# Last FFN of a decoder: quantisation cut in two steps, its scales on GpSimd, a bf16 last product, and the norm taken by halves

## The chip, the cores and the metric

The kernel is one program on 1 core of one Trainium2 chip. The metric is the time of one execution on the device, in microseconds; the figure for a kernel is the median of several runs. The kernel before took 2508.41 us (three runs, 2505.84 to 2514.92).

## The reference, cut to what matters

The model is a decoder of four layers, each with self-attention, cross-attention and an FFN, on 8 batches of 112 tokens with 256 features. The change touches the last FFN, in which inputs, weights and the hidden values are rounded to a 4-bit format with a scale for every 16 neighbouring elements:

```python
def fake_quant_nvfp4(x, global_scale):
    xb = x.reshape(sh[:-1] + (sh[-1] // BLOCK, BLOCK))          # BLOCK = 16
    amax = jnp.max(jnp.abs(xb), axis=-1, keepdims=True)
    sc = jnp.clip(amax / FP4_MAX * global_scale, 0.0, FP8_MAX)
    sc8 = sc.astype(jnp.float8_e4m3fn).astype(jnp.float32)
    dq = sc8 / global_scale
    safe_dq = jnp.where(dq == 0.0, 1.0, dq)
    a = jnp.clip(jnp.abs(xb) / safe_dq, 0.0, FP4_MAX)
    q = jnp.sign(xb) * _FP4_VALS[jnp.digitize(a, _FP4_MIDS)]
    return (q * dq).reshape(sh)
...
gate_out = nvfp4_linear(x, gate_w, s_in[0])                      # 256 -> 1024
up_out = nvfp4_linear(x, up_w, s_in[0])                          # 256 -> 1024
hidden = jax.nn.silu(gate_out) * up_out
return nvfp4_linear(hidden, down_w, s_in_down[0])                # 1024 -> 256
...
x = x + _L3_xattn_ref(_layernorm(x, axis=-1), ctx_512, L3_xattn_Wq, L3_xattn_Wkv, L3_xattn_Wo)
x = x + _L3_ffn_ref(_layernorm(x, axis=-1), L3_ffn_gate_w, L3_ffn_up_w, L3_ffn_down_w, L3_ffn_s_in, L3_ffn_s_in_down)
```

## The kernel before

The program runs the twelve sublayers one after the other on one core. The residual `x` stays in on-chip memory (SBUF) with the 112 tokens on partitions and (batch, feature) along the row. Each sublayer is written batch by batch or half by half (a half is four batches). Python code emits the instructions; a scheduler then sets the order on each engine by its own estimates, except on engines named in a `manual_schedule` block, where the order of the code stands. Every engine works through its own queue in order and waits on semaphores for the others. `self.t(pool, ..., tag)` takes a buffer from a pool; a tag has as many buffers as its pool's `bufs`, so a new one waits until the oldest is free.

The parts that matter here:

- `quantise` (from L1807) rounds `n` columns of `src` into `dst`. For each block of 16 columns it takes the largest magnitude (L1824), and then makes the scale from it in nine small instructions on n/16 columns: scale and clip (L1826, L1827), rounding to fp8 by masking the exponent and adding and subtracting a large number (L1831, L1834 to L1836), a guard against zero (L1837), the reciprocal (L1838) and its product with the global scale (L1840). Seven passes over all `n` columns follow: the quotient (L1843), clip (L1844), rounding (L1846 to L1849), and the product with the scale (L1850). All of it is on VectorE. A block's 16 elements are neighbours in the row.
- `l3_weights` (from L1852) does the same with the three weight matrices, in six calls on 1024 columns. It is a generator that `l2_ffn` (from L1607) advances while its own matmuls run; the rounded matrices are transposed on TensorE (L1884) and kept in bf16. Their raw values come by DMAs from GpSimd's queue (L1860). In `l2_ffn` VectorE also makes the gated product `hT` (L1625).
- `l3_xattn` (from L1798) is the cross-attention in front of the last FFN. It calls `cross` (from L950), whose order on TensorE, VectorE and ScalarE is written by hand. At the end of a batch it adds the result to `x` (L455).
- `l3_ffn` (from L1899): the norm of all of `x` (L1916, whose instructions carry the lines of the helpers `stats`, `rsqrt` and `normalise`: L402, L403, L385 to L392, L416), then for each half `quantise` on 1024 columns into `xq`, eight transposes (L1926), and a copy of the result to SBUF on ScalarE (L1931). After this comes a loop over four pairs of batches. For each pair, four times (two batches, two blocks of 512 columns): four matmuls into one `gu` buffer (a PSUM tile of which there are two; line L378 of the helper `mm`), Silu on ScalarE into `sg` (L1942), and the gated product into `hid` on VectorE (L1943). The pair's 2048 columns of `hid` are rounded into `hq` by one call of `quantise` (L1948), and for each batch eight transposes (L1952), a copy on ScalarE to `hqT` (L1956), eight matmuls into `y` (L378) and the sum with `x` (L1960) follow. Nothing in `l3_ffn` has an order by hand: the scheduler mixes pairs.
- `store` (L1963) writes `x` out with one DMA.

## Time and profile before

| what | before |
|---|---|
| runs, median (lowest to highest) | 2508.41 us (2505.84 to 2514.92) |
| the profiled execution's own time | 2510.18 us |
| its span, from first to last instruction | 2508.4 us |
| TensorE (PE) busy | 2223.4 us, 89% |
| VectorE (DVE) busy | 1460.0 us, 58% |
| ScalarE (ACT) busy | 834.6 us, 33% |
| GpSimd (POOL) busy | 212.9 us, 8% |
| granted TensorE clock, mean | 0.933 |
| last sum of the layer before the last FFN ends (L455) | 2384.4 us |
| last sum of the last FFN ends (L1960) | 2502.5 us |

The profile is one execution taken by the hardware profiler. It names engines PE (TensorE matmul), PEld (TensorE weight load), DVE (VectorE), ACT (ScalarE), POOL (GpSimd) and SP. Times are microseconds from the first instruction, durations in the group rows are mean nanoseconds. In a group row the first number is the total busy time, the second the mean of one instruction, and the last part is how long the engine sat idle just before such instructions and what ended that wait. Tiles have the names of the program. A row of the waits view reads: who waited, for whom, total us, number of times, longest.

### The profile page before, as it was taken

What the parts mean: (1) busy time and instruction counts of PE and PEld (TensorE: products, weight loads), DVE (VectorE), ACT (ScalarE), POOL (GpSimd) and SP (SyncE); (2) the same over time, 40 slices, a digit from 0 to 9 for tenths busy, and PEclk for the clock granted to TensorE, in tenths of its full rate; (3) what the DMA queues carried; (4) which work ended last, traced back from release to release, by engine and by line L of the source; (5) the groups of instructions that cost most, each with busy time, mean ns of one, the idle gap of its engine ahead of it and who ended that gap; (6) DMA issues with size and microseconds to landing.
All of it is one profiled execution on the core that took longest, in us unless ns stands there. A gap on an engine that the chain in (4) does not pass through costs nothing.

```text
span 2508.4 us, 43509 instructions
## 1 busy us (share of the span) xinstructions
PE 2223.4 (89%) x17192; PEld 1343.6 (54%) x17192; DVE 1460.0 (58%) x3879; ACT 834.6 (33%) x2276; POOL 212.9 (8%) x412
## 2 busy tenths in 40 slices
PE   6999999989989889999998887899999999799942
PEld 3444444657655656655666444456655556556622
DVE  4555656555544656763588664767660042656698
ACT  2333333111221246751012122367521111356621
POOL 0111111000001110000112231100000000100000
PEclk9999999786899999999999997999999999899966
DMA  4000001000010000001000001000111000000000
GB/s 182 2 2 2 2 19 63 1 17 1 17 51 1 14 18 2 18 18 42 34 1 34 18 18 59 34 2 1 52 51 50 35 17 1 1 1 2 2 0 15
DMA packets 10731, 56.42 MB, mean 22 GB/s; under 512 B 1833, under 2 KB 3625, under 8 KB 5536
## 3 DMA queue, kind: packets, MB, share of 16 engines
q1 hardware_dynamic: 8304, 45.03, 5.0%
q0 software_dynamic: 2080, 7.07, 0.8%
q8 instruction: 137, 2.24, 0.4%
q10 hardware_dynamic: 144, 1.54, 0.1%
q14 instruction: 66, 0.54, 0.1%
HBM read 52.69 MB, written 0.92 MB: 21 GB/s over the span
## 4 chain that ended last, share of the span: by engine, by line
PE 67%; DVE 21%; issue 5%; ACT 4%; DMA 1%; POOL 1%; DVEq 0%; ACTq 0%; POOLq 0%
PE mm L378 33%; PE gu L378 6%; PE g L612 6%; PE tr L1031 6%; PE sc L378 5%; PE av L378 3%; PE av L1047 2%; DVE xnm L1021 2%; DVE rot L1326 1%; ACT sg L623 1%; PE s L378 1%; ACT th L634 1%; DVE hT L638 1%; PE tr L477 1%; DVE h L636 1%
## 5 line engine op out<-in xcount | busy, mean ns | idle before, releaser
L612 PE MATMUL g<-w,hT 128*32 128x256 f32 x3552 | 237.4, 384 | 25.8 <-DVE hT L638 24.4
L1024 ACT ACTIVATE xe<-sc,xnm 112x375 f32<-112x375 f32 x384 | 215.6, 580 | 29.1 <-DVE xnm L1021 29.1
L1031 PEld LDWEIGHTS tr<-cst,xe 112*125 112x125 f32 x1152 | 157.2, 187 | 108.8 <-ACT xkT L982 30.0
L378 PE MATMUL mm<-xnT,w 128*128 128x448 f32 x432 | 191.3, 580 | 20.3 <-DVE qT L1329 4.5
L1031 PE MATMUL tr<-cst,xe 112*125 112x112 f32 x1152 | 197.8, 291 | 11.4 <-DVE xoT L1074 6.5
L1021 DVE TENSOR_REDUCE xnm<-sc 112x1 f32<-112x375 f32 x384 | 184.4, 541 | 29.2 <-PE sc L378 29.0
L378 PE MATMUL mm<-hT,w 128*128 128x448 f32 x512 | 193.0, 539 | 0.0
L612 PEld LDWEIGHTS g<-w,hT 128*32 128x32 f32 x3552 | 95.7, 109 | 167.5 <-DVE hT L638 124.6
L1039 DVE COPY xeT<-tr 125x336 f32<-125x336 f32 x192 | 97.4, 507 | 98.1 <-PE tr L1031 90.5
L378 PEld LDWEIGHTS mm<-hT,w 128*128 128x128 f32 x512 | 97.1, 190 | 94.4 <-issue 94.4
L378 PEld LDWEIGHTS mm<-xnT,w 128*128 128x128 f32 x432 | 80.5, 199 | 109.1 <-issue 55.8
L590 PE MATMUL g<-xw,cst 128*32 128x256 f32 x1792 | 138.7, 379 | 0.0
L378 PE MATMUL mm<-w,oT 128*112 128x256 f32 x416 | 119.8, 445 | 21.2 <-DVE oT L1506 13.7
L378 PE MATMUL mm<-w,hT 128*112 128x256 f32 x576 | 132.6, 389 | 0.0
L1037 ACT COPY xeT<-tr 125x336 f32<-125x336 f32 x192 | 85.3, 444 | 127.6 <-PE tr L1031 127.6
L378 PE MATMUL gu<-xnT,w 128*128 128x448 f32 x320 | 124.4, 544 | 1.7 <-DVE hT L1171 1.2
L378 PEld LDWEIGHTS mm<-w,hT 128*112 128x112 f32 x576 | 103.6, 182 | 27.6 <-issue 4.9
L378 PEld LDWEIGHTS mm<-w,oT 128*112 128x112 f32 x416 | 82.9, 208 | 52.4 <-DVE oT L1506 14.9
L623 ACT ACTIVATE sg<-g 128x192 f32<-128x192 f32 x224 | 74.2, 331 | 105.2 <-PE g L612 93.4
L634 ACT ACTIVATE th<-cell 128x64 f32<-128x64 f32 x224 | 57.7, 258 | 147.0 <-DVE cell L632 146.9
L455 DVE TENSOR_TENSOR x<-mm,x 112x256 f32<-112x256 f32 x64 | 27.1, 423 | 126.2 <-PE mm L378 126.2
L636 DVE TENSOR_TENSOR h<-sg,th 128x64 f32<-128x64 f32 x224 | 50.4, 225 | 84.9 <-ACT th L634 84.9
(375 smaller groups left out, 3744.5 us busy)
## 6 DMA issues: line engine op xcount, KB each, us to landing
w<-in_w SPq DMA_DIRECT2D x35, 1024.0 KB, 4.9
raw<-in_wq POOLq DMA_DIRECT2D x3, 1024.0 KB, 5.2
wi<-in_wint POOLq DMA_DIRECT2D x3, 768.0 KB, 5.9
w<-in_w SPq DMA_DIRECT2D x2, 896.0 KB, 16.6
w<-in_w SPq DMA_DIRECT2D x2, 768.0 KB, 4.1
ctxT<-in_ctxT ACTq DMA_DIRECT2D x1, 1500.0 KB, 7.8
cx<-in_ctx POOLq DMA_DIRECT2D x1, 1500.0 KB, 20.9
w<-in_w SPq DMA_DIRECT2D x2, 512.0 KB, 3.5
```

The costliest lines, as they stand in the source:

```text
L378: self.nc.tensor.matmul(out, lhsT, rhs, start=i == 0, stop=i == len(pairs) - 1)
L590: nc.tensor.matmul(g[32 * j : 32 * j + 32, :], pick[:, t % 16, :], xw[:, l, t // 16, 256 * j : 256 * j + 256], start=True, stop=t == 0, sk ...
L612: nc.tensor.matmul(g[32 * j : 32 * j + 32, :], hT[l][:, c, :], whh[l][:, c, 256 * j : 256 * j + 256], start=False, stop=c == 1, skip_group ...
L623: nc.scalar.activation(sg[:, :192], g[:, :192], AF.Sigmoid)
L634: nc.scalar.activation(th, cell[l], AF.Tanh)
L636: nc.vector.tensor_tensor(h, og, th, ALU.mult)
L1021: nc.vector.tensor_reduce(nm, sc, AX.X, ALU.max, negate=True)
L1024: nc.scalar.activation(e, sc, AF.Exp, bias=nm, accum_out=sums[b][:, at : at + 1])
L1031: nc.tensor.transpose(tp[:CH, i * S : (i + 1) * S], e[:, i * CH : (i + 1) * CH], self.ident[:S, :S])
L1037: nc.scalar.copy(eT, src)
L1039: nc.vector.tensor_copy(eT, src)
L1047: nc.tensor.matmul(avs[b][32 * j : 32 * j + 32, c * S : (c + 1) * S], values[b % 2][:CH, i, 4 * c + j, :], eTs[b, c, j][:, i, :], start=i ...
```

## The change

`quantise` becomes a generator with one stop in the middle: the first step makes the scales, the second does the passes over all columns. Of the small instructions the two that scale and clip, three of the four that round to fp8, and the last product with the global scale go to GpSimd, which also makes a copy of the scale in bf16; the exponent mask, the zero guard and the reciprocal stay on VectorE. The results of the passes are stored with a row's blocks interleaved ("at a pitch"): element e of all blocks, then element e+1. The same is done to the weights, so that the matmuls contract in the same permuted order. The last subtraction then writes bf16, and the product with the scale has only bf16 operands, with the scale repeated along the middle axis. The signs of the subtraction are turned round on both sides.

In `l3_ffn` the norm is taken half by half, just ahead of that half's quantisation. The loop over pairs becomes two functions: `hidden(b0)` makes `hid` and runs the first step of its quantisation, `result(b0)` runs the second step and the down projection. VectorE's order in this loop is written by hand: the hidden values and scales of the next pair, then the sums that are left of the last pair, then the quotient of the present one.

```diff
--- before.py
+++ after.py
@@ -1804,50 +1804,60 @@
             )
         w.done("l3x_wo")
 
-    def quantise(self, pool, src, dst, rows, n, gs, amax=None):
+    def quantise(self, pool, src, dst, rows, n, row, gs, amax=None, small=None):
 
 
         nc = self.nc
         nb = n // 16
 
-        def blocks(a):
-            return a.rearrange("p (k e) -> p k e", e=16)
+        def inner(a):
+            return a.rearrange("p (r e k) -> p r e k", e=16, k=row // 16)
 
         def bc(a):
-            return a[:, :, None].to_broadcast([rows, nb, 16])
-        def sm(tag):
-            return self.t(pool, [P, nb], f"q{tag}{nb}")[:rows]
+            return a.rearrange("p (r k) -> p r k", k=row // 16)[:, :, None, :].to_broadcast(
+                [rows, n // row, 16, row // 16]
+            )
+        def sm(tag, dt=F32):
+            return self.t(small or pool, [P, nb], f"q{tag}{nb}", dt)[:rows]
 
         if amax is None:
             amax = sm("m")
-            nc.vector.tensor_reduce(amax, blocks(src), AX.X, ALU.max, apply_absolute_value=True)
-        sc, st, z = sm("s"), sm("t"), sm("z")
-        nc.vector.tensor_scalar(sc, amax, 1.0 / 6.0, gs, ALU.mult, ALU.mult)
-        nc.vector.tensor_scalar(sc, sc, 448.0, None, ALU.min)
+            blocks = src.rearrange("p (k e) -> p k e", e=16)
+            nc.vector.tensor_reduce(amax, blocks, AX.X, ALU.max, apply_absolute_value=True)
+        sc, st, z, s16 = sm("s"), sm("t"), sm("z"), sm("h", BF16)
+        nc.gpsimd.tensor_scalar(sc, amax, 1.0 / 6.0, gs, ALU.mult, ALU.mult)
+        nc.gpsimd.tensor_scalar(sc, sc, 448.0, None, ALU.min)
 
 
         big = 1.5 * 2.0**23
         nc.vector.tensor_scalar(
             st.bitcast(I32), sc.bitcast(I32), 0x7F800000, None, ALU.bitwise_and
         )
-        nc.vector.tensor_scalar(st, st, 0.125 * big, 2.0**-9 * big, ALU.mult, ALU.max)
-        nc.vector.tensor_tensor(sc, sc, st, ALU.add)
-        nc.vector.tensor_tensor(sc, sc, st, ALU.subtract)
-        nc.vector.scalar_tensor_tensor(z, sc, 0.0, sc, ALU.is_equal, ALU.add)
+        nc.gpsimd.tensor_scalar(st, st, 0.125 * big, 2.0**-9 * big, ALU.mult, ALU.max)
+        nc.gpsimd.tensor_tensor(sc, sc, st, ALU.add)
+        nc.gpsimd.tensor_tensor(sc, st, sc, ALU.subtract)
+        nc.gpsimd.tensor_copy(s16, sc)
+        nc.vector.scalar_tensor_tensor(z, sc, 0.0, sc, ALU.is_equal, ALU.subtract)
         nc.vector.reciprocal(z, z)
 
-        nc.vector.tensor_scalar(z, z, gs, 1.0 + 2.0**-23, ALU.mult, ALU.mult)
+        nc.gpsimd.tensor_scalar(z, z, gs, 1.0 + 2.0**-23, ALU.mult, ALU.mult)
+        yield
         a = self.t(pool, [P, n], f"qa{n}")[:rows]
         m = self.t(pool, [P, n], f"qm{n}")[:rows]
-        nc.vector.tensor_tensor(blocks(a), blocks(src), bc(z), ALU.mult)
+        nc.vector.tensor_tensor(
+            inner(a), src.rearrange("p (r k e) -> p r e k", e=16, k=row // 16), bc(z), ALU.mult
+        )
         nc.vector.tensor_scalar(a, a, 6.0, -6.0, ALU.min, ALU.max)
 
         nc.vector.tensor_scalar(m.bitcast(I32), a.bitcast(I32), 0x7F800000, None, ALU.bitwise_and)
         nc.vector.tensor_scalar(m, m, 1.0, 0.5 * big, ALU.max, ALU.mult)
         nc.vector.tensor_tensor(a, a, m, ALU.add)
-        nc.vector.tensor_tensor(a, a, m, ALU.subtract)
-        nc.vector.tensor_tensor(blocks(dst), blocks(a), bc(sc), ALU.mult)
+        nc.vector.tensor_tensor(dst, m, a, ALU.subtract)
+        nc.vector.tensor_tensor(inner(dst), inner(dst), bc(s16), ALU.mult)
 
     def l3_weights(self, pool, ps):
 
@@ -1874,7 +1884,9 @@
             flat = wqs[i].rearrange("p o k -> p (o k)")
             for h in range(2):
                 cols = slice(h * 1024, (h + 1) * 1024)
-                self.quantise(pool, raws[i][:, cols], flat[:, cols], P, 1024, gs, amax[:, h * 64 : (h + 1) * 64])
+                am = amax[:, h * 64 : (h + 1) * 64]
+                for _ in self.quantise(pool, raws[i][:, cols], flat[:, cols], P, 1024, nk * P, gs, am):
+                    pass
 
         def turned(i, nk, no):
             out = self.wq[i].rearrange("p (k n) -> p k n", k=nk)
@@ -1913,13 +1925,14 @@
             nc.vector.reciprocal(inv[:, 1:2], s_down)
             for i, j in enumerate((0, 0, 1)):
                 nc.vector.tensor_tensor(sc[:, i : i + 1], self.igs[:, i : i + 1], inv[:, j : j + 1], ALU.mult)
-            self.normalise(self.x, self.xn)
             xq = self.t(acts, [P, NB, D], "xq", BF16)
             xqT = self.t(acts, [P, 2, T], "xqT", BF16)
             for half in range(2):
                 bs = slice(half * HB, (half + 1) * HB)
+                self.normalise(self.x[:, bs, :], self.xn[:, bs, :], n=HB)
                 flat = [a[:S, bs, :].rearrange("p b d -> p (b d)") for a in (self.xn, xq)]
-                self.quantise(pool, *flat, S, HB * D, s_in[:S])
+                for _ in self.quantise(pool, *flat, S, HB * D, D, s_in[:S]):
+                    pass
                 tp = self.t(ps, [P, 2, HT], "tr16", BF16)
                 for kc in range(2):
                     for j in range(HB):
@@ -1929,7 +1942,10 @@
                             self.ident16[:S, :S],
                         )
                 nc.scalar.copy(xqT[:, :, half * HT : (half + 1) * HT], tp)
-            for b0 in range(0, NB, 2):
+            quotients, hqs = {}, {}
+            def hidden(b0):
                 hid = self.t(work, [P, 2, 1024], "hid")[:S]
                 for j in range(2):
                     xb = self.tokens(b0 + j, xqT)
@@ -1943,21 +1959,39 @@
                         nc.vector.scalar_tensor_tensor(
                             hid[:, j, cols], gu[:S, 1, :], sc[:S, 1:2], sg, ALU.mult, ALU.mult
                         )
-                hq = self.t(work, [P, 2, 1024], "hq", BF16)[:S]
-                flat = [a.rearrange("p b d -> p (b d)") for a in (hid, hq)]
-                self.quantise(pool, *flat, S, 2048, s_down[:S])
+                hqs[b0] = self.t(work, [P, 2, 1024], "hq", BF16)[:S]
+                flat = [a.rearrange("p b d -> p (b d)") for a in (hid, hqs[b0])]
+                quotients[b0] = self.quantise(pool, *flat, S, 2048, 1024, s_down[:S], small=work)
+                next(quotients[b0])
+            def result(b0):
+                next(quotients[b0], None)
                 for j in range(2):
                     tp = self.t(ps, [P, 8, S], "tr16", BF16)
                     for c in range(8):
                         nc.tensor.transpose(
-                            tp[:, c, :], hq[:, j, c * P : (c + 1) * P], self.ident16[:S, :S]
+                            tp[:, c, :], hqs[b0][:, j, c * P : (c + 1) * P], self.ident16[:S, :S]
                         )
                     hT = self.t(work, [P, 8, S], "hqT", BF16)
                     nc.scalar.copy(hT, tp)
                     y = self.t(ps, [P, 512], "y")[:S, :D]
                     self.mm(y, [(hT[:, c, :], d[:, c, :]) for c in range(8)])
+                    yield
                     x = self.x[:S, b0 + j, :]
                     nc.vector.scalar_tensor_tensor(x, y, sc[:S, 2:3], x, ALU.mult, ALU.add)
+            with tc.manual_schedule(engines={ET.DVE}):
+                hidden(0)
+                last = iter(())
+                for b0 in range(0, NB, 2):
+                    if b0 + 2 < NB:
+                        hidden(b0 + 2)
+                    for _ in last:
+                        pass
+                    last = result(b0)
+                    next(last)
+                for _ in last:
+                    pass
 
     def store(self, out):
         self.nc.sync.dma_start(out.rearrange("b s d -> s b d"), self.x[:S])
```

## The prediction

> **What bounds the kernel now.** The page's 40 slices came first: in the last two PE falls to 4 and 2 tenths while DVE rises to 9 and 8. So I asked the table by stretches from the last residual sum of the layer before (L455, ends at 2384.4) to the last sum of this one (L1960, ends at 2502.5). The columns are length, then PE, PEld, DVE, ACT and POOL busy, and the granted TensorE clock:
>
> ```profile
> 2384.40:2401.30 16.90, 0.00 (x0) 0.00 (x0) 15.81 (x35) 0.21 (x1) 0.00 (x0) 0.62 0.00 0
> 2401.30:2423.90 22.60, 14.81 (x56) 7.63 (x57) 21.66 (x35) 9.75 (x13) 0.00 (x0) 0.73 0.01 1
> 2423.90:2445.30 21.40, 10.65 (x48) 6.89 (x48) 20.91 (x24) 4.46 (x6) 0.00 (x0) 0.63 0.00 0
> 2445.30:2466.90 21.60, 8.99 (x40) 6.11 (x39) 21.08 (x23) 3.09 (x4) 0.00 (x0) 0.60 0.00 0
> ```
>
> VectorE is the bound of the last 118.1 us: full but for some 0.5 us a stretch, GpSimd empty, TensorE under half busy at a clock of 0.60 to 0.63. Then VectorE's timeline, for how it is kept full (start, length):
>
> ```profile
> 2426.26 1.23 DVE L1844 TENSOR_SCALAR qa<-qa 112x2048 f32<-112x2048 f32 x1
> 2427.41 0.74 DVE L1943 SCALAR_TENSOR_TENSOR hid<-gu,sc,sg 112x512 f32<-112x512 f32 x1
> 2428.07 1.22 DVE L1846 TENSOR_SCALAR qm<-qa 112x2048 int32<-112x2048 int32 x1
> 2429.20 0.74 DVE L1943 SCALAR_TENSOR_TENSOR hid<-gu,sc,sg 112x512 f32<-112x512 f32 x1
> ```
>
> The four gate products of the next pair (L1943) each lie between two passes of this pair's quantisation. That gives TensorE and ScalarE 1.8 us for the next `gu`, of which PSUM holds two. The waits show the reverse side: others wait for VectorE, not it for them.
>
> ```profile
> PE tr L1952 <- DVE hq L1850: 37.0, 4, 13.9
> PE gu L378 <- DVE hid L1943: 17.8, 6, 7.1
> DVE hid L1943 <- ACT sg L1942: 0.3, 1, 0.3
> ```
>
> Last the prices, from the groups kept apart by shape (total, mean ns):
>
> ```profile
> L1850 DVE TENSOR_TENSOR hq<-qa,qs 112x2048 bf16<-112x2048 f32 x4 | 9.2, 2292 | 0.1
> L1844 DVE TENSOR_SCALAR qa<-qa 112x2048 f32<-112x2048 f32 x4 | 4.9, 1224 | 0.1
> L909 POOL TENSOR_SCALAR wide<-xri 112x512 f32<-112x512 f32 x8 | 12.0, 1496 | 80.4 <-DVE xri L907 72.1 <-DVE nt L389 8.3
> L1062 POOL COPY xrw<-xri 112x512 f32<-112x512 f32 x24 | 14.8, 615 | 537.1 <-PE av L1047 342.5 <-DVE xri L1060 194.6
> ```
>
> **What the Trainium skill says.** "VectorE: DVE Perf Modes", section on the perf-mode tier table: a `tensor_tensor` of 2048 fp32 takes 2293 ns, of bf16 in SBUF 1224. The trace agrees with the first (2292, L1850); no row of before shows a bf16 one. "GPSIMD Engine Reference", section 3.1: elementwise work on GpSimd costs about twice VectorE's; the trace is worse at small sizes, below. "SBUF — State Buffer", section "Who interferes with whom": a VectorE instruction with two SBUF inputs and a GpSimd one that reads SBUF block each other. The trace agrees: the same 256-column product on VectorE runs 0.41 us alone and up to 0.95 beside GpSimd (L1368). "TensorE: Matmul & The Clock Gate", Part 1: after idling, TensorE starts at half rate for some 3.4 us. The trace agrees: eight `gu` matmuls took 3.66 us after a 5.6 us pause, four in a running burst 1.02.
>
> **The change, part by part.**
>
> *Removed from VectorE.* Per pair of batches six of the nine small scale steps leave (L1826 0.28, L1827 0.22, L1834 0.23, L1835 0.29, L1836 0.29, L1840 0.28: 1.59 us). The last product becomes bf16 throughout with step 1 innermost; I take the page's 1.22 for 2.29, saving 1.07 (bounds 0 and 1.07). Sum 2.66, four times: 10.6. Per half of the input, with 1024 columns: 1.35 of small steps, and 0.53 of the product (1.22 to 0.69, the size that L1844 has at 1024 columns in two-a-cycle mode): 1.9, twice: 3.8. Normalising by halves takes four L416 off the path, 1.3. **Together 15.7.** The first product now reads at a stride of 16 in fp32; I take it as unchanged (2.29), as is the subtraction into bf16 (L1850 already writes bf16 at that price).
>
> *(a) Added: VectorE waits for GpSimd.* VectorE's order in this stage is now written by hand, and in the built order of the instructions nothing stands between maximum, exponent mask (old L1831), zero test (old L1837) and reciprocal. So VectorE sits through two GpSimd instructions, then through three. Their price is not in the trace at 128 columns. GpSimd's sum takes 0.72 at 256 columns (L1410, least loaded) and 1.13 at 448 (L1330): 2.15 ns a column, 0.17 fixed. L909's 1.49 at 512 with the same fixed part is 2.6 a column. Estimates at 128: 0.50 (scalar form), 0.44 (sum); at 64: 0.34 and 0.31. Below, the copy's rate (L1062, L639) gives 0.30; above, twice the slope for two operations, 0.80. Handing over from VectorE to GpSimd took 0.08 (L1329 to L1330), and I take 0.07 between GpSimd's own dependent steps. First wait 2x0.50+0.23 = 1.23, second 0.50+2x0.44+0.30 = 1.68: 2.91 a pair, 2.2 for pair 0 where the input's last product hides part, 10.9 in all. The two halves add 1.8 and 2.6. **Sum 15.3.** Queued behind: everything on VectorE, so every gate product and quotient. The bf16 copy of the scales and the last GpSimd product run under the quotient of the pair before; without that cover they would cost 0.8 a pair.
>
> *(b) Added: gate products bare.* They now follow each other with nothing between. Two `gu` are ready; the third needs the buffer freed by the first, and in TensorE's built order stand before it eight transposes of the quotient just finished (0.94, L1952), and inside it eight `y` matmuls, which wait for ScalarE's copy. From that quotient's end: 0.94 + 1.37 (three quarters of 1.83) + 1.6 (eight `y`, between 0.9 and 1.97 by clock) + 0.26 + hand-overs 0.2 + 0.69 (`sg`) = 5.1. VectorE has done two products by 1.55: it waits 3.6, and 0.4 at the fourth. That holds for pairs 2 and 3 (4.0 each); pair 1, without transposes in the way, waits 2.0 + 1.1; pair 0 0.5. **Sum 11.6.**
>
> *(c) Added: the sums of pair 2 stand before the quotient of pair 3.* VectorE waits out transposes, copy and `y`, as it does at the very end today (4.03 + 0.41): **4.3**. Today that lies under L1843.
>
> *(d) Lost overlap.* In the mixed order independent neighbours start 0.09 before the other ends (L1844 1.23 long, next start 1.15 later); a bare dependent chain leaves 0.03 between. The built order carried through with these durations gives **2.5** for this, the remainder.
>
> Tail: 15.3+11.6+4.3+2.5-15.7 = **+18.0**. By stretch: first `xq` at 2397.4 (before 2401.3), `hq` of the four pairs at 2444.5, 2471.2, 2497.9, 2515.2 (before 2439.1, 2460.5, 2480.0, 2497.1), last sum 2520.5 (2502.5).
>
> *(e) Norm of the first half* now runs inside the attention layer before. Its square root needs ScalarE to switch tables and back there: 2x1.28 + 0.21 = 2.8 us in a period of 5.0 in which ScalarE is busy 3.6 (14.3 of 20) and TensorE 4.9 (19.6 of 20). ScalarE can absorb 1.4; the rest, with VectorE's ten extra instructions, delays exponentials that TensorE waits for: **+1.6** (0 to 3).
>
> *(f) The same routine for the weights*, under the layer-L2 FFN: six halves, each 1.9 less VectorE work and about 2.5 of waits. TensorE is 50.0 of 50 us busy there and reads these weights up to 95 us later: 0. Uncovered it would be some 4 us. The sharpest place is a gate product (L1625) behind a 4.4 us chain where 6.0 are allowed by two buffers. The load of the next raw weights queues behind fifteen GpSimd instructions, but is used later still. I take 0, -0.5 to 2.
>
> Sum: +19.6 on the profiled execution (span 2508.4, its own time 2510.2): 2529.8. The runs' median, 2508.4, is 1.8 below that execution, so **2528.0**.
>
> **Rivals.**
> 1. *GpSimd near its floor* (0.30 and 0.35): the chain gives 2516.4, so +13.9+1.6: 2524; with TensorE at full clock as well 2517. For: the scalar row is a broadcast, perhaps dear. Against: the clock row of 0.6.
> 2. *Not slower by anything measurable.* One mechanism: the waits on GpSimd in (a) vanish, because its instructions of 64 and 128 columns cost little more than VectorE's own 0.2. Place: the two waits of each chain. Price: the 15.3 of (a) goes, and +4.3 remains, 2512.7. It decides from GpSimd instructions of about 0.2 us down, where less than half of (a) is left. Against: 0.22 already for 16 columns (L639).
> 3. *GpSimd dear* (0.80 and 0.60, two operations and a scalar from memory): the chain gives 2528.0, so 2535.6.
> 4. *The bf16 product isn't faster*, the change not doing what it says: +4.9 on mine, 2533.
>
> **Chances.** Forecast 55%, its own range 2520 to 2534; rival 1 14%, rival 2 11%, rival 3 13%, rival 4 7%. The range 2513 to 2540 leaves out about 1 in 10 at each end: it reaches below from rival 1 to rival 2, above past rival 3 with (e) and (f) at their high ends. Some 0.5% (12.5 us) is what a measurement of this kernel tells from no change. Slower by more: forecast, 3, 4 and about a third of rival 1: 0.80. Within: the rest of rival 1 and most of 2: 0.16. Faster: 0.04, the mechanism of 2 with a full TensorE clock on top and errors of mine.
>
> **What would show it.** Right: VectorE waiting for GpSimd around 15 us, with GpSimd's rows at 0.4 to 0.6; a third gate product per pair that waits 3 to 4 us for `sg`; about 4 us before the sums of pair 2; a pair period near 26.7 us instead of 21.6; last product at 1.2; the first `xq` earlier by 4. Wrong: GpSimd rows at 0.2, a pair period under 23, or TensorE gaps growing in the attention layer by more than 3 us.

## The result and the profile after

| | before | after |
|---|---|---|
| median of the runs beside each other | 2508.67 us (2505.84 to 2514.92, 4 runs) | 2534.07 us (2533.54 to 2534.65, 4 runs) |
| span of the profiled execution | 2508.4 us | 2532.8 us |
| its own time | 2510.18 us | 2534.65 us |
| last sum before the last FFN ends (L455) | 2384.4 us | 2385.8 us |
| last sum of the last FFN ends (L1981, old L1960) | 2502.5 us | 2526.7 us |

The ratio is 1.010, 95% interval 1.0087 to 1.0112: slower by 25.4 us, where 19.6 were forecast. The last FFN takes 140.9 us instead of 118.1, so 22.8 of the 24.2 us between the two ends arise there.

The stretches of the last FFN in the kernel after, cut at the ends of `xq` and of the four `hq` (columns as in the table shown of before):

```profile
2419.30:2446.80 27.50, 6.37 (x16) 2.99 (x15) 20.68 (x18) 2.75 (x4) 7.63 (x10) 0.56 0.00 1
2446.80:2474.40 27.60, 8.59 (x48) 5.92 (x48) 20.29 (x18) 4.45 (x6) 3.26 (x7) 0.62 0.00 0
2474.40:2501.80 27.40, 6.63 (x40) 4.88 (x40) 20.23 (x17) 3.07 (x4) 3.26 (x7) 0.62 0.00 0
2501.80:2520.50 18.70, 4.58 (x32) 4.10 (x32) 13.97 (x10) 1.71 (x2) 0.00 (x0) 0.59 0.00 1
```

A pair of batches takes 27.5 us instead of 21.5. VectorE's busy time (third pair of numbers) hardly fell, from some 21.0 to 20.3 a pair; what is new is some 7 us in each pair (6.8 to 7.3) in which it stands still, where it stood 0.5. Its waits in this stretch, in the kernel after:

```profile
DVE hid L1959 <- ACT sg L1958: 11.6, 6, 3.8
DVE x L1981 <- PE y L378: 9.7, 4, 4.0
DVE qz L1844 <- POOL qs L1842: 9.7, 6, 1.8
DVE qt L1837 <- POOL qs L1833: 6.2, 6, 1.2
DVE qa L1851 <- POOL qz L1847: 0.9, 2, 0.5
```

Three rows are GpSimd (16.8 us), one the gate products, one the sums. VectorE's timeline from the end of the first quotient on, in the kernel after, shows where they stand:

```profile
2445.55 1.23 DVE L1860 TENSOR_TENSOR hq<-hq,qh 112x2048 bf16<-112x2048 bf16 x1
2446.70 1.40 DVE L1959 SCALAR_TENSOR_TENSOR hid<-gu,sc,sg 112x512 f32<-112x512 f32 x2
2451.93 0.75 DVE L1959 SCALAR_TENSOR_TENSOR hid<-gu,sc,sg 112x512 f32<-112x512 f32 x1 [3.84 <-ACT sg L1958]
2452.88 0.75 DVE L1959 SCALAR_TENSOR_TENSOR hid<-gu,sc,sg 112x512 f32<-112x512 f32 x1 [0.20 <-ACT sg L1958]
2453.67 2.29 DVE L1830 TENSOR_REDUCE qm<-hid 112x128 f32<-112x2048 f32 x1
2457.11 0.23 DVE L1837 TENSOR_SCALAR qt<-qs 112x128 int32<-112x128 int32 x1 [1.16 <-POOL qs L1833]
2459.18 0.29 DVE L1844 SCALAR_TENSOR_TENSOR qz<-qs 112x128 f32<-112x128 f32 x1 [1.84 <-POOL qs L1842]
2459.51 0.95 DVE L1845 RECIPROCAL qz<-qz 112x128 f32<-112x128 f32 x1
2460.38 0.78 DVE L1981 SCALAR_TENSOR_TENSOR x<-y,sc,x 112x256 f32<-112x256 f32 x2
2461.07 3.60 DVE L1851 TENSOR_TENSOR qa<-hid,qz 112x2048 f32<-112x2048 f32 x1
```

Two gate products go at once, the third waits 3.84, and no quotient pass stands between them any more. Then the chain sits out GpSimd twice, 1.16 and 1.84. The last line is what the forecast didn't have: the first product of the quotient takes 3.60. The groups by shape of the kernel after give its mean, and those of the last product and of GpSimd's steps:

```profile
L1851 DVE TENSOR_TENSOR qa<-hid,qz 112x2048 f32<-112x2048 f32 x4 | 14.3, 3575 | 0.0
L1851 DVE TENSOR_TENSOR qa<-xn,qz 112x1024 f32<-112x1024 f32 x2 | 3.7, 1872 | 0.9 <-POOL qz L1847 0.9
L1860 DVE TENSOR_TENSOR hq<-hq,qh 112x2048 bf16<-112x2048 bf16 x4 | 4.9, 1224 | 0.1
L1840 POOL TENSOR_SCALAR qt<-qt 112x128 f32<-112x128 f32 x4 | 2.6, 652 | 1.4 <-DVE qt L1837 1.4
L1833 POOL TENSOR_SCALAR qs<-qs 112x128 f32<-112x128 f32 x4 | 2.2, 552 | 0.3
L1841 POOL TENSOR_TENSOR qs<-qs,qt 112x128 f32<-112x128 f32 x4 | 1.8, 452 | 0.3
```

The last product is as cheap as taken (1.22). The strided first product is not unchanged: 3.58 for 2.29, and 1.87 for 1.23 at 1024 columns.

### The profile page after: what moved, and what is told of

Read it like the earlier page. It is cut to its first block, busy times and chain, and to the rows that moved or that the text cites. A ratio compares the mean times of both kernels' runs of the same rounds, so it can differ in the third digit from the quotient of the medians.

```text
span 2532.8 us, 43547 instructions
## 1 busy us (share of the span) xinstructions
PE 2218.7 (88%) x17192; PEld 1343.2 (53%) x17192; DVE 1447.4 (57%) x3813; ACT 835.9 (33%) x2279; POOL 258.7 (10%) x496
## 4 chain that ended last, share of the span: by engine, by line
PE 68%; DVE 21%; ACT 4%; issue 4%; POOL 2%; DMA 1%; DVEq 0%; ACTq 0%; POOLq 0%
PE mm L378 34%; PE gu L378 6%; PE tr L1031 6%; PE g L612 6%; PE sc L378 5%; PE av L378 3%; PE av L1047 2%; DVE xnm L1021 2%; DVE rot L1326 1%; ACT sg L623 1%; PE s L378 1%; ACT th L634 1%; DVE hT L638 1%; DVE h L636 1%; DVE cell L632 1%
## 5 line engine op out<-in xcount | busy, mean ns | idle before, releaser
L378 PE MATMUL mm<-xnT,w 128*128 128x448 f32 x432 | 187.6, 571 | 19.6 <-DVE qT L1329 4.5
L455 DVE TENSOR_TENSOR x<-mm,x 112x256 f32<-112x256 f32 x64 | 27.1, 423 | 123.7 <-PE mm L378 123.7
```

What stands on the lines that cost most here:

```text
L378: self.nc.tensor.matmul(out, lhsT, rhs, start=i == 0, stop=i == len(pairs) - 1)
```

## The experiments

All medians are of runs beside runs of the kernel before, whose medians were 2509.1, 2508.9 and 2509.8 in the three sets.

| run | median us | ratio to before, 95% interval |
|---|---|---|
| e1_free_order | 2517.06 | 1.0028 (1.0016 to 1.0040) |
| e2_scales_vectore | 2530.93 | 1.0086 (1.0073 to 1.0100) |
| e3_blocks_as_before | 2534.56 | 1.0100 (1.0086 to 1.0113) |
| e4_turn_in_subtraction | 2569.97 | 1.0239 (1.0225 to 1.0253) |
| e5_norm_halves_only | 2506.49 | 0.9990 (0.9984 to 0.9996) |
| e6_weight_scales_gpsimd | 2517.53 | 1.0032 (1.0019 to 1.0044) |
| e7_two_steps_vectore | 2505.85 | 0.9985 (0.9978 to 0.9991) |
| e8_two_steps_scalare_pass | 2501.12 | 0.9966 (0.9953 to 0.9979) |
| e9_after_weights_vectore | 2535.14 | 1.0106 (1.0092 to 1.0119) |
| e10_free_activations_gpsimd | 2509.46 | 0.9996 (0.9988 to 1.0004) |
| e11_weights_no_all_reduce | 2519.48 | 1.0040 (1.0027 to 1.0052) |
| e12_scalare_and_halves | 2500.52 | 0.9964 (0.9951 to 0.9976) |

A whole run mixes several places, so each profile is also cut at instructions that all kernels share. A runs from the last L1369 (at about 1600) to the last L1404, the end of layer L2's cross-attention and its closing MLP, under which the first weight matrix is rounded; B to the last L1650, the end of the layer's FFN; C to the last L455, the end of the cross-attention ahead of the last FFN; the tail to the last sum. The lengths are worked out from the starts of these instructions. Ahead of A, where no kernel was changed, the profiles differ by up to 4.5 us:

| kernel | A | B | C | tail |
|---|---|---|---|---|
| before | 249.7 | 275.1 | 255.0 | 118.1 |
| after | 253.4 | 276.1 | 253.8 | 140.8 |
| e1 | 255.4 | 276.0 | 256.7 | 119.2 |
| e2 | 252.4 | 275.3 | 256.2 | 135.9 |
| e3 | 254.0 | 275.1 | 259.7 | 138.3 |
| e4 | 257.5 | 276.1 | 257.2 | 168.2 |
| e5 | 249.5 | 275.2 | 256.1 | 115.4 |
| e6 | 254.1 | 274.7 | 254.9 | 117.6 |
| e7 | 249.6 | 275.1 | 254.9 | 114.7 |
| e8 | 249.7 | 275.2 | 254.8 | 111.0 |
| e9 | 251.0 | 275.3 | 257.7 | 140.2 |
| e10 | 250.7 | 275.1 | 253.9 | 117.8 |
| e11 | 251.4 | 278.0 | 260.2 | 118.3 |
| e12 | 249.9 | 275.1 | 255.9 | 108.9 |

### e1: the order left to the scheduler

```diff
-            with tc.manual_schedule(engines={ET.DVE}):
+            if True:
```

> The changed kernel with one thing undone: VectorE's order in the last FFN is left to the scheduler instead of being written by hand. Reference points are the two medians, 2508.7 before and 2534.1 after. Theory (the loss is the waits of VectorE that the hand-written order creates, plus 6.4 for the strided quotient, less the work saved): in the freely built order the gate products, the scale steps and the residual sums lie between passes of another pair's quotient. So the 11.6 us of gate products waiting for ScalarE and the 4.5 us of the sums of the third pair go, and of the 16.8 us of waits for GpSimd only those of the two input halves and of the first pair stay, about 7. Expected 2534 - 11.1 - 4.5 - 9.8 = 2509, within 4. Rival A (GpSimd's share of the scales is dear wherever it stands): only the gate and sum waits go, 2518. Rival B (the layout is the whole cost, the order none): no change, 2534.

Measured: 2517.1, 17 less than the changed kernel. The tail fell from 140.8 to 119.2: the waits for gate products went from 11.6 to 1.0 and those ahead of the third pair's sums are gone, so the theory's main part stands. Rival B falls. But the total is at rival A's figure, 8 above the theory's. In the tail, VectorE still waits for GpSimd: 13.4 us instead of about 7. The timeline of this run's third pair shows why:

```profile
2456.16 1.25 DVE L1857 TENSOR_SCALAR qm<-qm 112x2048 f32<-112x2048 f32 x1
2456.42 1.39 POOL L1833 TENSOR_SCALAR qs<-qs 112x128 f32<-112x128 f32 x1
2457.98 2.28 DVE L1858 TENSOR_TENSOR qa<-qa,qm 112x2048 f32<-112x2048 f32 x1
2458.15 2.62 POOL L1840 TENSOR_SCALAR qt<-qt 112x128 f32<-112x128 f32 x1 [0.35 <-DVE qt L1837]
2461.87 0.29 DVE L1844 SCALAR_TENSOR_TENSOR qz<-qs 112x128 f32<-112x128 f32 x1 [1.61 <-POOL qs L1842]
```

L1840 takes 2.62 us where it took 0.65 in the kernel after: VectorE's two-input pass L1858, which was to cover it, started 0.17 earlier and shuts it out until it ends. VectorE then waits 1.61 for the steps behind it. Without that hold, L1840 and the two steps behind it (0.45 each) would have ended before L1858 does. L1833 is held up in the same way by L1857, which has only one input. In the first pair of this run L1840 takes 0.65 beside a gate product (L1959), which reads PSUM. This is the mutual block that the prediction names ahead of its sum, seen here with a one-input pass too; the prediction used it nowhere in its sum. The passes that are long enough to hide GpSimd's steps are the ones that stop them. In the kernel after, the hold shows with the weights: beside the quotient of each matrix's first half, L1840 of the second half takes 2.08 to 2.10 instead of 0.46.

The other part of the excess lies in A and C, 4.9 more than in the kernel after, with the same instructions in the same order on every engine. All six executions of e1 lie within 2 us of each other, so this is no matter of a single execution. What differs is the granted TensorE clock: from 200 to 250 us into A it is 0.93, in the kernel after 0.97 and in before 1.00. C differs in two stretches, from 14 to 37 and from 64 to 85 us behind the last L1650 (six kernels that all have the norm by halves):

| kernel | granted clock in the two stretches | C |
|---|---|---|
| after | 0.89, 1.00 | 253.8 |
| e10 | 0.88, 1.00 | 253.9 |
| e5 | 0.85, 0.89 | 256.1 |
| e1 | 0.85, 0.89 | 256.7 |
| e9 | 0.74, 0.85 | 257.7 |
| e3 | 0.73, 0.76 | 259.7 |

So C's differences of up to 6 us go with the clock; why the clock differs there was not settled.

### e2: the small scale steps on VectorE

```diff
-        nc.gpsimd.tensor_scalar(sc, amax, 1.0 / 6.0, gs, ALU.mult, ALU.mult)
+        nc.vector.tensor_scalar(sc, amax, 1.0 / 6.0, gs, ALU.mult, ALU.mult)
...
-        nc.gpsimd.tensor_copy(s16, sc)
+        nc.vector.tensor_copy(s16, sc)
```

> The changed kernel with the small scale steps on VectorE again, everything else as it is, the hand-written order too. Theory: the 16.8 us of waits for GpSimd go and 9.1 us of VectorE work come back (1.59 for each of four pairs, 1.35 for each of two halves), so 2534 - 7.7 = 2526; gate and sum waits stay near 11.6 and 4.5. Rival A (moving the scales to GpSimd is the whole loss): back to the time before, 2509. Rival B (GpSimd relieves VectorE, waits or not): slower by the 9, 2543.

Measured: 2530.9, 3.1 less; the tail is 4.9 shorter, where 7.7 was expected. The expectation left out that the bf16 copy of the scales moves too (about 0.2 each time, 1.3 in all), and the waits for gate products and sums grew by 0.9. GpSimd is no longer waited for, yet most of the loss stays. Rival A (GpSimd is the whole loss) falls, and so does rival B: under the hand-written order, taking the work off VectorE costs more than it frees. The strided quotient is as long as before, with GpSimd doing nothing in the last FFN:

```profile
L1851 DVE TENSOR_TENSOR qa<-hid,qz 112x2048 f32<-112x2048 f32 x4 | 14.4, 3598 | 0.0
```

### e3: blocks laid out as before

```diff
-            inner(a), src.rearrange("p (r k e) -> p r e k", e=16, k=row // 16), bc(z), ALU.mult
+            inner(a), inner(src), bc(z), ALU.mult
...
-        nc.vector.tensor_tensor(dst, m, a, ALU.subtract)
-        nc.vector.tensor_tensor(inner(dst), inner(dst), bc(s16), ALU.mult)
+        nc.vector.tensor_tensor(a, m, a, ALU.subtract)
+        nc.vector.tensor_tensor(inner(dst), inner(a), bc(sc), ALU.mult)
```

Here `inner` and `bc` are the contiguous `blocks` and `bc` of before.

> The changed kernel with the layout of before: quotient and last product on contiguous blocks of 16, the last product from fp32 with fp32 scales, no bf16 copy of the scales. Theory: the quotient falls from 3.58 to 2.29 at 2048 columns (1.87 to 1.23 at 1024), -6.4 in the last FFN, and the last product rises from 1.22 to 2.29 (0.68 to 1.22), +5.4: the two halves of the layout change nearly cancel, 2533, that is a difference of -1 us within 1.5. Rival A (the strided quotient is long only because GpSimd runs beside it): the quotient stays at 3.5 and the product rises, 2539.5. Rival B (the layout is the whole loss): towards 2509.

Measured: 2534.6, no difference; the tail is 2.5 shorter (1.0 expected; the gate products' waits are another 1.5 less). The quotient fell with GpSimd's steps in place:

```profile
L1852 DVE TENSOR_TENSOR qa<-hid,qz 112x2048 f32<-112x2048 f32 x4 | 9.1, 2268 | 0.0
```

So rival A falls, and rival B with it. The layout change alone is a trade: the strided product gives back what the bf16 product wins.

### e4: the reordering in the subtraction

```diff
-            inner(a), src.rearrange("p (r k e) -> p r e k", e=16, k=row // 16), bc(z), ALU.mult
+            blk(a), blk(src), z[:, :, None].to_broadcast([rows, nb, 16]), ALU.mult
...
-        nc.vector.tensor_tensor(dst, m, a, ALU.subtract)
+        nc.vector.tensor_tensor(turn(dst), rke(m), rke(a), ALU.subtract)
```

> The changed kernel with the reordering moved: the quotient reads and writes contiguous blocks, and the subtraction that rounds, whose result is bf16 already, reads both fp32 inputs in order and writes at the pitch; the last product stays bf16 with step 1. Theory 1 (only a strided fp32 read is dear, a strided bf16 write is not): quotient 2.29 for 3.58, subtraction unchanged at 2.29, so -6.4: 2527.7. Theory 2 (any access at this stride costs VectorE 1.3 us per 2048 columns): the cost moves to the subtraction, 2534. No number of before speaks for either; I lean to theory 1 by 6 to 4.

Measured: 2570.0. Both theories missed by far. The groups by shape of this run:

```profile
L1868 DVE TENSOR_TENSOR hq<-qm,qa 112x2048 bf16<-112x2048 f32 x4 | 37.1, 9278 | 0.1
L1868 DVE TENSOR_TENSOR xq<-qm,qa 112x1024 bf16<-112x1024 f32 x2 | 8.9, 4455 | 0.0
L1860 DVE TENSOR_TENSOR qa<-hid,qz 112x2048 f32<-112x2048 f32 x4 | 9.1, 2267 | 0.0
```

The quotient is back at 2.27, and the subtraction that writes bf16 at a pitch takes 9.28 instead of 2.29 (4.46 for 1.22 with half the columns). A strided read costs 0.6 ns more an element here, a strided bf16 write 3.4 more (7.0 us by 2048). The changed kernel has its reordering in the cheaper of the two places. With the source's order e3 and e4 also turn back the way in which the scale is repeated in the quotient, so the 0.6 was not measured for the strided source alone; the last product repeats its scale in the new way in bf16 and takes 1.22.

### e5: the norm by halves alone

```diff
-            self.normalise(self.x, self.xn)
...
+                self.normalise(self.x[:, bs, :], self.xn[:, bs, :], n=HB)
```

> The kernel before with one part of the change alone: the norm by halves. In the trace after, the stretch from the sum of the sixth batch of the cross attention to the last sum grew by 1.1 us against before, in four other kernels that also have the halves by 1.1 to 1.2 too, and one half's four normalising instructions (1.3) leave the path in the last FFN. Theory: +1.1 - 1.3, with some start-up work of the norm gone as well: 2508.7 within 1. Rival (the early norm is a real gain, the attention hides it): 2506 or below.

Measured: 2506.5, 2.4 less, near the rival's figure. The tail is 2.7 shorter, since not only four L416 but also the square root and its refinement for the first half have left it, and C is 1.1 longer. This part of the change is a small gain.

### e6: the weights' scale steps on GpSimd alone

```diff
+        eng = eng or nc.vector
-        nc.vector.tensor_scalar(sc, amax, 1.0 / 6.0, gs, ALU.mult, ALU.mult)
+        eng.tensor_scalar(sc, amax, 1.0 / 6.0, gs, ALU.mult, ALU.mult)
...
-                self.quantise(pool, raws[i][:, cols], flat[:, cols], P, 1024, gs, amax[:, h * 64 : (h + 1) * 64])
+                self.quantise(pool, raws[i][:, cols], flat[:, cols], P, 1024, gs, amax[:, h * 64 : (h + 1) * 64], nc.gpsimd)
```

> The kernel before with one part of the change alone: the six small scale steps on GpSimd for the weights, not for the activations. The prediction took this as hidden (0). In the trace after, VectorE waits 2.6, 1.4, 0.4 and 0.2 us for GpSimd with the first matrix while the sums of the recurrent layer's feed-forward (L1597, L1404) queue behind, and TensorE then stands 2.8 us waiting for one of these sums. Theory: this costs time, about 2 to 4 us of the 3.7 by which that stretch grew (the longer quotient has the rest): 2511.7. Rival (the prediction's: TensorE reads these weights much later, nothing is lost): 2508.7.

(The sums L1597 and L1404 belong to the closing MLP of layer L2's cross-attention, not to the recurrent layer's feed-forward.) Measured: 2517.5, 8.7 more. The profiled executions stand only 4.4 apart (spans 2512.8 and 2508.4), so the profile can place about half of this. The prediction's "hidden" falls. A is 4.4 longer, and this is also where the changed kernel lost 3.7. GpSimd's timeline in the kernel after:

```profile
1809.64 0.38 POOL L1879 PARTITION_ALL_REDUCE gs<-top  x1 [7.50 <-issue]
1816.96 0.31 POOL L1832 TENSOR_SCALAR qs<-amax,gs 128x64 f32<-128x64 f32 x1 [6.94 <-issue]
```

VectorE's timeline meanwhile, in the kernel after:

```profile
1813.61 0.43 DVE L1597 TENSOR_TENSOR xo<-mm,xo 112x256 f32<-112x256 f32 x1 [3.21 <-PE mm L378]
...
1817.81 0.20 DVE L1837 TENSOR_SCALAR qt<-qs 128x64 int32<-128x64 int32 x1 [2.63 <-POOL qs L1833]
1819.38 0.23 DVE L1844 SCALAR_TENSOR_TENSOR qz<-qs 128x64 f32<-128x64 f32 x1 [1.38 <-POOL qs L1842]
...
1821.05 1.87 DVE L1851 TENSOR_TENSOR qa<-raw,qz 128x1024 f32<-128x1024 f32 x1 [0.23 <-POOL qz L1847]
1822.84 0.41 DVE L1597 TENSOR_TENSOR xo<-mm,xo 112x256 f32<-112x256 f32 x1
```

and TensorE's:

```profile
1823.31 5.30 PE L378 MATMUL mm<-w,hT 128*112 128x256 f32 x16 [2.83 <-DVE xo L1597]
```

GpSimd ends the all-reduce at 1810.0 and starts the scale step, whose input is there at 1810.4, only at 1817.0. In these 6.9 us nothing is shown that it waits for. VectorE, which takes its instructions in order, stands behind it, the second sum of the MLP comes 9.2 us after the first instead of 3.3 (1818.74 to 1822.02 in before), and TensorE waits 2.83 for the buffer that this sum frees. After this wait TensorE is granted 0.68 of its clock from 1824 to 1828, where before has 1.00. The Trainium skill, "GPSIMD Engine Reference", section 2.1, says that the first call of freshly loaded code on GpSimd pays a load of about 6 us that no instruction in the profile shows. The trace agrees in kind: such a gap of 6.9 to 7.0 stands ahead of all three first scale steps after an all-reduce, and e11 below tests what it costs. Whether it is such a load is not shown.

### e7: two steps, all on VectorE

```diff
+        yield
         a = self.t(pool, [P, n], f"qa{n}")[:rows]
...
+            quotients, hqs = {}, {}
+            def hidden(b0):
...
+            def result(b0):
+                next(quotients[b0], None)
```

The loop is the changed kernel's, without the hand-written order; the small buffers come from `work`, of which there are two.

> The kernel before with one part of the change alone: quantisation in two steps over two pairs of batches, with separate small buffers, built freely, all of it on VectorE, blocks as before. Theory (the two steps are good when nothing waits): the small scale steps of the next pair lie between passes of this one, so independent neighbours overlap by 0.09 instead of standing 0.03 apart, some 8 of 13 instructions in three pairs: about 0.12 x 24 = 2.9 us less, 2505.8. Rival A (two pairs' gate products first delay the first quotient and nothing is won back): 2509 to 2512. Rival B (two steps are what slows the changed kernel): 2515 or more.

Measured: 2505.9, as the theory says; the tail is 3.4 shorter, and both rivals fall. Worked out from the starts and lengths of VectorE's instructions in the tail, their overlap with each other grew from 4.4 to 6.7 us, 2.3 of the 3.4, so the theory's mechanism is seen as well. Two steps over two pairs were not what hurt.

### e8: one pass on ScalarE

```diff
-            nc.vector.tensor_scalar(m, m, 1.0, 0.5 * big, ALU.max, ALU.mult)
-            nc.vector.tensor_tensor(a, a, m, ALU.add)
-            nc.vector.tensor_tensor(a, a, m, ALU.subtract)
+            nc.scalar.activation(m, m, AF.Relu, scale=0.5 * big, bias=shift[:rows])
+            nc.vector.scalar_tensor_tensor(a, m, 0.5 * big, a, ALU.add, ALU.add)
+            nc.vector.scalar_tensor_tensor(m, m, 0.5 * big, a, ALU.add, ALU.subtract)
```

`shift` holds -0.75 x 2^23. The subtraction's sign is turned in the scale, as in the changed kernel.

> As the kernel with the two steps on VectorE, and one pass of 2048 columns (maximum with 1, times 0.75 x 2^23) of the first three pairs moved to ScalarE as a ReLU with scale and bias, the missing constant added in the two passes that follow, same result. ScalarE is busy 3 to 4 of 21.6 us there. Its 512-column gate activation takes about 0.7 us, so I estimate 2.0 to 2.5 for 2048. Theory (moving work off VectorE pays when it goes to an engine that VectorE's passes don't hold up and other VectorE work covers the latency): 1.22 less for each of three pairs, 3.7 less than the two-step kernel: 2502. Rival (a wait takes its place, as with GpSimd): VectorE waits 1 us or more for ScalarE in each pair and the gate activations queue behind the long pass: no gain over the two-step kernel, or a loss of 1 to 3.

Measured: 2501.1, 4.7 less than e7, with the tail 3.7 shorter, three times the 1.22 of the pass that left. The timeline of this run's second pair:

```profile
2444.31 1.22 DVE L1852 TENSOR_SCALAR qm<-qa 112x2048 int32<-112x2048 int32 x1
2445.56 2.00 ACT L1858 ACTIVATE qm<-qm,shift 112x2048 f32<-112x2048 f32 x1 [2.29 <-DVE qm L1852]
2445.58 0.74 DVE L1962 SCALAR_TENSOR_TENSOR hid<-gu,sc,sg 112x512 f32<-112x512 f32 x1
2446.44 0.74 DVE L1962 SCALAR_TENSOR_TENSOR hid<-gu,sc,sg 112x512 f32<-112x512 f32 x1
2447.62 2.29 DVE L1859 SCALAR_TENSOR_TENSOR qa<-qm,qa 112x2048 f32<-112x2048 f32 x1
```

ScalarE needs 2.00 for it in each of the three pairs, VectorE fills that time with two gate products and scale steps of the next pair, and no wait stands ahead of L1859. The rival falls. The change's aim, less work on VectorE, was sound; it needed an engine that VectorE's passes don't block and an order that covers the latency.

### e9: the weights' scale steps back on VectorE, in the changed kernel

```diff
+        eng = eng or nc.gpsimd
...
-                for _ in self.quantise(pool, raws[i][:, cols], flat[:, cols], P, 1024, nk * P, gs, am):
+                for _ in self.quantise(pool, raws[i][:, cols], flat[:, cols], P, 1024, nk * P, gs, am, eng=nc.vector):
```

> The changed kernel with the weights' scale steps on VectorE again; activations, order and layout as changed. Theory: the part that the weights cost goes (3.7 us in the stretch that holds the first matrix and 1.0 in the one after it, by the two traces; only the longer quotient, 0.65 twice for the first matrix, stays): 2534 - 3.7 = 2530.4, within 1.5. Rival (the weights are hidden, as the prediction had it, and what the stretch lost is chance): 2534.

Measured: 2535.1: the total doesn't move, and by it the theory is not confirmed. Yet A is 2.4 and B 0.8 shorter, as expected, though A's own spread (2.0 between e1 and after) weakens that. C is 3.9 longer, with nothing changed in it; the surplus lies in the two stretches of the table under e1, at a lower granted clock. So what A gave, C took, and C's loss goes with the clock.

### e10: activations on GpSimd, order free, the rest as before

The edits of e1, e3 and e9 together.

> The changed kernel with order built freely, blocks as before, and weights' scale steps on VectorE: what is left of the change is two steps, norm by halves, and the activations' scale steps on GpSimd. Theory (GpSimd is held up by the pass of VectorE that is to cover it: in the freely built run its 0.65 step took 2.62 beside a pass with two inputs from SBUF, and VectorE then waited 1.6): the tail is that run's 119.2 less 1.0 for the layout, against 114.7 with two steps on VectorE; 2509, within 2. Rival (once the order is free the work taken off VectorE is won): two steps and halves give 2503.5, less 1.59 for each of four pairs: 2497.

Measured: 2509.5, at the theory's figure; the rival's 2497 is far outside. The tail is 117.8 against e7's 114.7, although e10 has the norm by halves, worth 2.7 there; VectorE waits 13.6 us for GpSimd. Even in a free order the activations' steps on GpSimd cost some 5.8 us in the tail against VectorE doing them.

### e11: no all-reduce ahead of the weights' steps

```diff
-            nc.gpsimd.partition_all_reduce(gs, top, P, bass_isa.ReduceOp.max)
+            nc.gpsimd.tensor_copy(gs, top)
```

> The kernel before with the weights' scale steps on GpSimd, as run before, and the maximum over partitions left out: each partition scales with its own maximum, a GpSimd copy stands where the all-reduce stood. In every trace GpSimd's first scale step after an all-reduce starts some 7 us late with nothing that it waits for shown, and a first such gap of 7.5 to 7.7 stands ahead of the all-reduce. Theory (GpSimd pays about 7 us to change between these two kinds of instruction, and VectorE's sums wait behind): the gap goes, and with it most of the 8 us that the weights' steps cost: 2509 to 2511. Rival (the steps themselves and their hand-overs cost it): 2516 to 2517.

Measured: 2519.5: the total speaks for the rival, the stretches don't. GpSimd starts the first scale step 0.5 after the copy, and A falls from e6's 254.1 to 251.4, 2.7 of the 4.4. But with the all-reduce the gap ahead of it went too, and that one stands in before as well: 7.66 us with nothing shown that it waits for, ahead of the first matrix's all-reduce, behind which VectorE waits 5.65. (Ahead of the third the same idle time is a wait for VectorE's maximum, and e11 has it too, 7.68.) So the 2.7 belongs to both gaps together. But B and C grew by 3.3 and 5.3. The sixth to the seventh sum of the cross-attention (L455) took 25.9 us where e6 and before have 18.4, and the table by stretches of this run shows what was different there:

```profile
2350.00:2360.00 10.00, 9.63 (x102) 6.64 (x101) 7.09 (x16) 7.07 (x23) 0.00 (x0) 1.00 0.01 2
2360.00:2370.00 10.00, 9.03 (x89) 6.40 (x90) 5.76 (x15) 6.54 (x21) 0.62 (x1) 0.82 0.01 2
2370.00:2380.00 10.00, 9.88 (x69) 6.10 (x73) 5.46 (x12) 3.67 (x12) 0.00 (x0) 0.50 0.01 2
2380.00:2390.00 10.00, 8.67 (x66) 6.61 (x66) 3.31 (x13) 4.77 (x12) 0.62 (x1) 0.66 0.00 0
```

TensorE was 87 to 99% busy and was granted down to half its clock (the column after GpSimd's), in a place where all other kernels have 1.00 up to 2380. So the total is no verdict on GpSimd's gap. By A alone the two gaps together would account for more than half of what the weights' steps cost there; with A's spread of 2 that is a hint and not shown.

### e12: e8 with the norm by halves

The edits of e8 and e5 together.

> The kernel with two steps on VectorE and the pass on ScalarE (2501.1), with the norm by halves as well. Theory (gains of separate causes add): 2501.1 - 2.4 = 2498.7, ratio to before 0.996. Rival (the halves' gain was the same idle time that the two steps use): 2501.

Measured: 2500.5. The tail is 2.1 shorter than e8's and C 1.1 longer; the difference of 0.6 in the medians is too small to tell the theory from the rival. The version beats both kernels: 0.9964 of the time before (0.9951 to 0.9976).

## Why the prediction was right, and where it was not

The side, the place and the mechanism were right: VectorE, the bound, was given waits in a tail that had none. In the profiled executions the forecast was +19.6, and the ends stand 24.2 apart; the median, 2534.1, lies at the upper edge of the forecast's own range, 2520 to 2534. By its steps:

| step | forecast | measured | by |
|---|---|---|---|
| removed from VectorE | -15.7 | -17.1 | last product 1.22; the halves take 2.7 from the tail (e5), not 1.3 |
| first product at a stride | 0 | +6.4 | 1.28 x 4 + 0.65 x 2 (L1851; e2, e3) |
| (a) waits for GpSimd | +15.3 | +16.8 | the three rows of waits |
| (b) bare gate products | +11.6 | +11.6 | the row of L1959 |
| (c) sums of pair 2 first | +4.3 | +5.3 | 4.5, and 0.8 more at the very last sum |
| (d) lost overlap | +2.5 | -0.2 | what is left of 22.8 |
| (e) norm in the attention | +1.6 | +1.1 | the periods of L455; e5 |
| (f) weights | 0 | +4.7 | A and B |

With 2.1 less ahead of A and 2.3 less in C apart from (e), neither of them touched by the change, this is 24.2. That these 4.4 us nearly cancel the 4.7 of (f) is luck.

The tail can also be taken apart without the forecast's steps. From before to after, VectorE's durations in it sum to 11.0 us less (17.4 of work gone, 6.4 of stride added), their overlap shrinks by 1.4, the gaps under 0.15 us between them shrink by 1.6 and the longer ones grow by 33.9. This makes the 22.7 by which the tail grew.

- **The step that failed** is the sentence "I take it as unchanged (2.29)". The quotient's stride was seen, and no row of before priced it; its bound from above was left at zero. It measured 6.4 us, more than the whole miss of 4.6; the other errors partly cancel. The Trainium skill, "SBUF — State Buffer", section "Door 1: The DMA port swizzle", says that SBUF is read in lines of 16 bytes and that each step to a new line costs; the prediction should have drawn on this for its upper bound. The trace agrees in direction: 1.56 times the time for a read in steps of 64 bytes.
- **(f) failed** because the prediction looked at where TensorE is full (1900 to 2100). The first matrix is rounded earlier, at 1810 to 1840, beside an MLP whose sums TensorE waits for, and GpSimd's 7 us gap after the all-reduce was not in the sum. A and B show 4.7; A is 249.5 to 250.7 in the six kernels with the weights' steps on VectorE and blocks as before, and 253.4 to 255.4 in the four with GpSimd and no strided write, so this is more than A's spread. The strided quotient has a share too: with the weights' steps on VectorE and the stride kept, A is 252.4 (e2) and 251.0 (e9). The two don't add up, since A is no shorter without the stride (254.0 in e3, 254.1 in e6). How much of (f) reaches the end is open: e6 alone costs 8.7 in total, e9 recovers nothing, and C varies from 253.8 to 260.2 between kernels that hardly differ there.
- **(a) was right in size**: the five GpSimd steps of the two waits mostly took 0.37 to 0.65 at 128 columns against 0.44 and 0.50 estimated. That GpSimd is worse than twice VectorE at small sizes holds for two of them alone, 0.65 for 0.23 (L1840) and 0.55 for 0.23 (L1833); the sums took 0.45 for 0.29.
- **(b)** was right to 0.1: 3.84 and 0.20 for the third and fourth product, 3.6 and 0.4 forecast. e1 and e7 show that it comes from the hand-written order alone.
- **(d)** was right in kind and too large: the lost overlap is 1.4, and the 1.6 of small gaps that went with the moved instructions hide it in the remainder of -0.2.
- **The rivals.** GpSimd near its floor, GpSimd dear, and waits that vanish are all excluded by its rows; the bf16 product that isn't faster by 1.22. What rival 4 would have cost (4.9; the savings that it loses, 1.07 x 4 and 0.53 x 2, make 5.3) came by another way, the stride. The pair period was 27.5, 26.7 forecast.

## What to carry to other kernels

When the engine that bounds a stage is relieved, ask of each moved instruction who then waits for whom in the order as built: here 15.7 us of work were to leave VectorE, and some 33 us of waits came. Work is moved to an engine that the bound engine's passes don't shut out, and its latency is laid under independent work, as the pass on ScalarE was. A pass whose access pattern changes is priced anew even if its element count stays, reads and writes apart.

## What the runs showed of the hardware that was not expected

- A two-input fp32 product on VectorE with one input in steps of 64 bytes takes 3.58 us at 2048 columns instead of 2.29; the same size with a strided bf16 result takes 9.28.
- A GpSimd step of 128 columns (L1840) takes 0.65 us alone and 2.62 when a two-input VectorE pass of 2.28 starts first (e1); beside a gate product that reads PSUM it keeps its 0.65.
- GpSimd's first elementwise step after an all-reduce over partitions starts 6.9 to 7.0 us behind it, with nothing shown that it waits for; behind a copy in the same place it starts 0.5 behind (e11).
- The granted TensorE clock fell to 0.50 under full load in one kernel (e11), where one batch of the cross-attention took 25.9 us for 18.4. At the start of the last layer it was 0.73 to 0.89 in kernels whose instructions there are the same, and C is up to 6 us longer where it is lower. Why it falls at these points was not settled.
- A ReLU of 2048 fp32 columns on ScalarE took 2.00 us, where VectorE's pass for the same took 1.22.
